# A selective scan in tiles of (state, channel) instead of (channel, state)

## The chip, the cores and the metric

The kernel runs on one core of a Trainium2 chip. The metric is the device time of one execution in microseconds, the median of several runs; for the kernel before it is 7444.82 us over 3 runs (7441.77 to 7446.32). A profiled execution of the same program gives the trace that is read below.

## The reference

Two layers follow each other on an image batch x of shape (4, 128, 128, 128), all in float32. The change lies in the first, a Mamba-like block over the L = 16384 pixels of each image:

```python
h1 = jax.nn.relu(xf @ mlp_w1.T + mlp_b1)
xm = h1 @ mlp_w2.T + mlp_b2
x_in, z = jnp.split(xm @ in_proj_w.T, 2, axis=-1)
u = silu(causal depthwise conv of x_in, 4 taps, + conv_b)      # 256 channels
dt, Bm, Cm = jnp.split(u @ x_proj_w.T, [8, 24], axis=-1)       # 16 states
delta = jax.nn.softplus(dt @ dt_proj_w.T + dt_proj_b)
A = -jnp.exp(A_log)
def step(h, inp):
    d_t, B_t, C_t, u_t = inp
    dA = jnp.exp(d_t[:, :, None] * A)
    h = h * dA + d_t[:, :, None] * B_t[:, None, :] * u_t[:, :, None]
    y = jnp.einsum('bds,bs->bd', h, C_t)
    return (h, y)
y = (ys + u * D) * silu(z)
out = y @ out_proj_w.T          # then group norm over 4 groups, silu, + x
```

So for each of 256 channels d and 16 states s there is a recurrence along the pixels. The second layer (a group norm, a small mixing head, and a filter in the Fourier domain) is not touched.

## The kernel before

`block0` is the first layer, `block1` the second. An image is cut into 32 chunks of T = 512 pixels, so there are 128 chunks for the four images, one after the other. Within a chunk the 256 x 16 = 4096 recurrences are 32 tiles of 128 partitions: a tile holds DG = 32 channels and SQ = 4 states, and partition p is channel p // 4 and state p % 4. Two halves j of 128 channels have four groups of 32 channels each (index m or g) and four groups of four states (index p in the code). A step r of a half takes, for each state group p, the channel group `place(r, p)`, so a step covers all four channel groups, each with another state group.

The recurrence itself is one VectorE instruction per tile along the pixels (L409, a scan of 128x512). It needs two operands:

- da = exp(delta * A), made by ScalarE (L391) from `rdelta`, which holds delta repeated over the four states, with a per-partition scale `amat`.
- b = delta * u * B. For state groups 1 to 3 GpSimd multiplies `rdu` (delta * u repeated over four states) by `rB` (B repeated over 32 channels) into `hb` (L358, `dbu`). For state group 0 it is made on another way: the product du is turned by TensorE so that pixels are on partitions (L288), ScalarE scales it by the four B values of the pixel (L299, `bt_act`, a per-partition scale), which writes the tile `bt`, and TensorE turns a 128-column piece of `bt` back into the PSUM tile b (L378, `dbu_turn`).

The scan result is multiplied by `rC` (C repeated over the channels), on VectorE in place (L411) or on GpSimd (L416), and TensorE sums the four states of each channel with the 0/1 matrix `sel` (L430). ScalarE keeps the last column of each scan for the next chunk (L412, L417).

The repeated tiles come through DRAM. `xd_act` stores B and C as `bc` (L250), `bc_load` reads them back into `rB` and `rC` (L257); `dt_act` stores delta (L272) and `du_pool` stores du (L308) into `dd`, and `rep_load(j)` reads them back into `rdelta` and `rdu` (L315). A load in this kernel fills one group of all 128 partitions, with a source that is repeated: `replicated` repeats each channel's row four times, and `partition_broadcast(DG)` repeats four state rows 32 times. `rB`, `rC`, `rdelta` and `rdu` have two buffers each; `rdelta` and `rdu` are used in turn by the two halves of a chunk.

The order of the work is written out by hand. Time is cut into slots, 16 to a chunk (NP), one for each pair of scans. The list at the end of `pre(k)` and that of `post(k)` give each piece of work of chunk k a slot and a phase, counted from the slot where chunk k - 1 begins its scans; chunk k itself begins at slot 16. In a slot the phases run in the order turn, sums, pe, exps, act, pool, dbu, gate, scans, dve, end. Chunk k's `bc` is stored in slot 4, `rB` and `rC` loaded in slot 5, delta stored in 6, du made and stored in 7, the first half's `rdelta` and `rdu` loaded in 9, and the second half's in 16. `dbu` runs two slots ahead of its scans (the first of a chunk in slot 14), `exps` one slot ahead (15). ScalarE's `bt` work is spread over slots 8 to 14. All these transfers are issued by SP, in that order, from one queue.

For images 0 to 2 the group norm, and after it the mixing head of the second layer (`finish`), run in the chunks of the next image: `norm_load`, `norm_act` and `norm_dve` in 16 of the 32 chunks (L561, L562, L567, L571), `agg_load` and its matmul (L593, L597) in most of the chunks after those.

Of the kernel before, what the change touches and what calls it, by code (L numbers as in the profile page):

```python
# [26 lines left out]
F32 = mybir.dt.float32  # L27
AF = mybir.ActivationFunctionType
# [5 lines left out]
P = 128  # L34
T = 512
DG = 32
SQ = 4
# [8 lines left out]
def kernel(ctx: ExitStack, tc: tile.TileContext, a: dict, out: bass.AP):  # L46
# [91 lines left out]
    stats, outs = {}, {}  # L138
    shared = SimpleNamespace(**{k: v for k, v in locals().items() if k not in ("ctx", "tc")})
    block0(tc, shared)  # L140
    block1(tc, shared)


def block0(tc, s):
    nc, B, NCH, NH, NS, NG, ND, R, NX, KC, HALO, C, L, NF, DI = (
        s.nc, s.B, s.NCH, s.NH, s.NS, s.NG, s.ND, s.R, s.NX, s.KC, s.HALO, s.C, s.L, s.NF, s.DI,
    )
    NT = T // P
    with ExitStack() as ctx:
        def pool(name, bufs, **kw):  # L150
            return ctx.enter_context(tc.tile_pool(name=name, bufs=bufs, **kw))

        p1 = pool("p1", 1)
        p2 = pool("p2", 2)
# [19 lines left out]
        st = {}  # L174
        stats, outs = s.stats, s.outs

        def replicated(ap):

            return ap.rearrange("d (o t) -> d o t", o=1).to_broadcast([DG, SQ, T])

        def pre(k):


# [2 lines left out]
            d = st[k] = {}  # L186
# [65 lines left out]
            def bc_load():  # L252
                for q, tag in enumerate("BC"):
                    t = d[tag] = p2.tile([P, NG - 1 + q, T], F32, tag=f"r{tag}", name=f"r{tag}_{k}")
                    for g in range(1 - q, NG):
                        rows = d["bc"][q, g * SQ : (g + 1) * SQ, :]
                        nc.sync.dma_start(out=t[:, g - 1 + q, :], in_=rows.partition_broadcast(DG))  # L257

            def dt_mm():
                for j in range(NH):  # L260
# [31 lines left out]
            def bt_act(h, n0, n1):  # L292

                if h == n0 == 0:
                    d["bt"] = p2.tile([P, NT, NH * ND, DG, SQ], F32, tag="bt", name=f"bt_{k}")
                for n in range(n0, n1):
                    t, q = divmod(n, SQ)
                    src = ps["dut"][:, 2 * t : 2 * t + 2, :].rearrange("p j (g d) -> p (j g) d", d=DG)
                    nc.scalar.activation(  # L299
                        d["bt"][:, 2 * h + t, :, :, q], src, AF.Copy, scale=d["xdt"][:, 2 * h + t, R + q : R + q + 1]  # L300
                    )

            def du_pool(j):
# [6 lines left out]
            def rep_load(j):  # L310
                for q, tag in enumerate(("delta", "du")):
                    t = d[tag, j] = p2.tile([P, ND, T], F32, tag=f"r{tag}", name=f"r{tag}_{k}_{j}")
                    for g in range(ND):
                        r = j * P + g * DG
                        nc.sync.dma_start(out=t[:, g, :], in_=replicated(d["dd"][q, r : r + DG, :]))  # L315

            return [
                (-9, "pe", load), (-7, "pe", h1_mm), (-6, "act", h1_act), (-5, "pe", xm_mm), (-4, "act", xm_act),
                (-3, "pe", z_mm), (-1, "act", z_act), (0, "pe", partial(cv_mm, 0)), (1, "pe", partial(cv_mm, 1)),
                (2, "act", silu_act), (3, "pe", xd_mm), (4, "act", xd_act), (5, "pe", dt_mm), (5, "pe", xd_turn),  # L320
                (5, "act", bc_load), (6, "act", dt_act), (7, "act", xd_turn_act), (7, "pool", partial(du_pool, 0)),
                (7, "pool", partial(du_pool, 1)), (8, "pe", partial(du_turn, 0)), (9, "act", partial(rep_load, 0)),
                (8, "pool", partial(bt_act, 0, 0, 1)), (9, "act", partial(bt_act, 0, 1, 5)),
                (10, "act", partial(bt_act, 0, 5, 8)), (11, "pe", partial(du_turn, 1)),
                (11, "pool", partial(bt_act, 1, 0, 1)), (12, "act", partial(bt_act, 1, 1, 2)),
                (13, "act", partial(bt_act, 1, 2, 5)), (14, "act", partial(bt_act, 1, 5, 8)),
                (16, "pe", partial(rep_load, 1)),
            ]

# [7 lines left out]
        def place(r, p):  # L337


            return (p - r) % ND  # L340
# [22 lines left out]
        def pair(n):  # L363

            k, r = divmod(n, NP)
            u, p = divmod(r, ND // 2)
            j, r = divmod(u, NG)
            return k, j, r, 2 * p

        def dbu_turn(n):  # L370

            k, j, r, p = pair(n)
            d = st[k]
            if p == 0:
                b = d["b0"] = psd.tile([P, T], F32, tag="b0", name=f"b0_{k}_{j}_{r}")
                for t in range(NT):
                    src = d["bt"][:, t, j * ND + place(r, 0), :, :].rearrange("p d s -> p (d s)")
                    nc.tensor.transpose(b[:, t * P : (t + 1) * P], src, s.ident)  # L378

        def exps(n):  # L380
# [104 lines left out]
        for n in range(n_chunks * NP):  # L485
            todo[n - 1, "exps"].append(partial(exps, n))
            todo[n - 1, "turn"].append(partial(dbu_turn, n))
            todo[n, "scans"].append(partial(scans, n))
            if n % 2 == 0:
                todo[n - 2, "dbu"].append(partial(dbu, n // 2))  # L490
            else:
                todo[n + 2, "sums"].append(partial(sums, n // 2))
# [400 lines left out]
def _layout(inputs):  # L893

    import numpy as np

    v = {k: np.asarray(x) for k, x in inputs.items()}
    p0 = {k[len("L0_conv_"):]: x for k, x in v.items() if k.startswith("L0_conv_")}
    p1 = {k[len("L1_conv_"):]: x for k, x in v.items() if k.startswith("L1_conv_")}
    _, C, H, W = v["x"].shape  # L900
    out = {
        "x": v["x"],
        "mlp_w1T": p0["mlp_w1"].T,
        "mlp_w2T": p0["mlp_w2"].T,
        "in_wT": p0["in_proj_w"].T,
        "conv_wT": p0["conv_w"][:, 0, :].T,

        "alog_q": p0["A_log"].reshape(2, 4, 32, 4, 4).transpose(2, 4, 0, 3, 1).reshape(128, 32),
        "x_wT": p0["x_proj_w"].T,
        "dt_wT": p0["dt_proj_w"].T,  # L910
        "dt_b": p0["dt_proj_b"],
        "out_wT": p0["out_proj_w"].T,
        "agg_wT": p1["agg_w"].T,
        "wg_wT": p1["wg_w"].T,
        "residual_weight": p1["residual_weight"].reshape(1),
    }
    for k in ("mlp_b1", "mlp_b2", "conv_b", "D", "gn_w", "gn_b"):
        out[k] = p0[k]
    for k in ("gn_gamma", "gn_beta", "agg_b", "wg_b", "filt_w"):
        out[k] = p1[k]  # L920

    def groups(n):
        g = np.arange(C) // (C // n)
        return (g[:, None] == g[None, :]) * (n / C)

    def angle(n, rows, cols):
        return 2 * np.pi * ((np.asarray(rows)[:, None] * np.asarray(cols)[None, :]) % n) / n

    h, w, k = np.arange(H), np.arange(W), np.arange(W // 2 + 1)
    ah, aw, ai = angle(H, h, h), angle(W, w, k), angle(W, k, w)  # L930

    half = np.concatenate([h[: H // 2 + 1], H + h[: H // 2 + 1]])
    rows = np.concatenate([h[: H // 2], h[: H // 2 - 1 : -1]])
    out["filt_w"] = out["filt_w"][:, :, rows]
    twice = np.where((k == 0) | (k == W // 2), 1.0, 2.0)[:, None]
    consts = {
        "c_ident": np.eye(C),
        "c_sel": np.repeat(np.eye(32), 4, axis=0),
        "c_g0": groups(4),

        "c_g1": groups(16),
        "c_fh": np.concatenate([np.cos(ah), -np.sin(ah)], 1)[:, half] / np.sqrt(H),
        "c_fwr": np.concatenate([np.cos(aw), -np.sin(aw)], 1) / np.sqrt(W),
        "c_fwi": np.concatenate([np.sin(aw), np.cos(aw)], 1) / np.sqrt(W),
        "c_ihc": np.cos(ah)[rows] / np.sqrt(H),
        "c_ihs": -np.sin(ah)[rows] / np.sqrt(H),
        "c_sign": np.tile(np.repeat([1.0, -1.0], H // 2), (W, 1)),
        "c_iw": np.concatenate([twice * np.cos(ai), -2.0 * np.sin(ai[1:-1])], 0) / np.sqrt(W),
    }
    out |= {k: np.asarray(x, np.float32) for k, x in consts.items()}  # L950
    return {k: np.ascontiguousarray(x) for k, x in out.items()}
# [18 lines left out]
```

## Time and profile before

| | |
|---|---|
| median of 3 runs | 7444.82 us |
| the profiled execution | 7446.74 us |
| its span | 7445.0 us, 90541 instructions |
| DMA packets | 853767, 1242.06 MB |
| VectorE scans (L409), 128x512 | 1268 ns (da from da, st, hb), 1271 ns (h from da, st, b) |
| VectorE product with rC (L411), 128x512 | 674 ns |
| GpSimd product (L358), 128x1536 / 128x1024 / 128x512 | 3447 / 2369 / 1279 ns |
| GpSimd product with rC (L416), 128x1024 | 2367 ns |
| ScalarE exp (L391), 128x512 | 696 ns |
| ScalarE eviction into bt (L299), 128x256 | 708 ns, 2048 of them |
| SP transfers rdelta / rdu / rC / rB | 1024 / 1024 / 512 / 384 of 256 KB |

A busy time counts the instructions of an engine, not its waits; an engine with a high share either sets the pace or stands close to it. A group of instructions shows its number, its total and the mean of one, and then the idle time ahead of them with what ended it. A transfer's time to landing runs from its issue to its completion and holds what was queued ahead of it. The scan stage covers the first 6500 us or so of the span; the second layer's stage is the rest.

### The profile page before, as it was taken

The numbers are of one execution on the slowest core, as the hardware profiler recorded it, in microseconds if no ns is written. First come the engines' busy times: TensorE is split into PE (matmuls) and PEld (weight loads), VectorE is DVE, ScalarE is ACT, GpSimd is POOL, SyncE is SP. The second block draws the span as 40 slices with busy tenths as digits, with TensorE's granted clock in tenths as the row PEclk, the third lists the DMA queues.
The fourth block names the chain that finished last, engine by engine and source line by source line (L and its number), as shares of the span: only waits on it lengthen the run. The fifth ranks groups of instructions, "written<-read, shape, count | busy, mean of one in ns | idle before, by whom it ended". The sixth has DMA issues, their size and how long they took to land.

```text
span 7445.0 us, 90541 instructions
## 1 busy us (share of the span) xinstructions
PE 6005.7 (81%) x25908; PEld 2664.1 (36%) x25908; DVE 7031.4 (94%) x8168; ACT 6328.6 (85%) x13181; POOL 6900.6 (93%) x3188
## 2 busy tenths in 40 slices
PE   7787878877778788887777788877777788867999
PEld 2223223322222233332222223232222233237999
DVE  6999999999999999999999999999999999977787
ACT  6888888888888888888888888888888888866887
POOL 6999999999999999999999999999999999976788
PEclk8888888888888888888888889988888889889999
DMA  4444444444554544544545454445554554547665
GB/s 138 159 154 150 151 156 156 143 161 168 174 188 164 179 165 156 169 166 169 184 168 185 161 171 166 159 165 175 171 188 166 173 169 151 173 149 216 177 185 155
DMA packets 853767, 1242.06 MB, mean 167 GB/s; under 512 B 76680, under 2 KB 308240, under 8 KB 853264
## 3 DMA queue, kind: packets, MB, share of 16 engines
q1 hardware_dynamic: 851152, 1236.11, 50.3%
q8 instruction: 204, 3.34, 0.2%
q14 instruction: 299, 2.45, 0.1%
q10 hardware_dynamic: 2112, 0.16, 0.0%
HBM read 992.71 MB, written 243.27 MB: 166 GB/s over the span
## 4 chain that ended last, share of the span: by engine, by line
ACT 20%; DVE 19%; PE 17%; POOL 9%; issue 8%; DMA 5%; SPq 1%; DVEq 0%; ACTq 0%; POOLq 0%
DVE da L409 8%; ACT da L391 8%; DVE h L409 6%; PE pp_cv L231 5%; ACT bt L299 4%; POOL hb L358 4%; POOL hb L416 4%; DVE hb L411 3%; DMA dd<-delta 2%; PE y L430 2%; PE pa L776 1%; ACT L391 1%; PE px L790 1%; PE px L791 1%; POOL du L307 1%
## 5 line engine op out<-in xcount | busy, mean ns | idle before, releaser
L358 POOL TENSOR_TENSOR hb<-rdu,rB 128x1536 f32<-128x1536 f32 (+2 forms) x1536 | 3607.6, 2365 | 16.2 <-DMA rdu<-dd 16.2
L416 POOL TENSOR_TENSOR hb<-h,rC 128x1024 f32<-128x1024 f32 (+1 forms) x1072 | 2438.7, 2277 | 279.8 <-DVE h L409 263.0
L391 ACT ACTIVATE da<-rdelta,amat 128x512 f32<-128x512 f32 x4096 | 2674.6, 696 | 9.2 <-ACT st L412 0.2
L409 DVE TENSOR_TENSOR_SCAN da<-da,st,hb 128x512 f32<-128x512 f32 x1976 | 2420.3, 1268 | 7.1 <-ACT da L391 7.0
L378 PE MATMUL b<-ident,bt 128*128 128x128 f32 x4096 | 768.9, 311 | 767.9 <-DVE h L409 633.0
L430 PE MATMUL y<-hb,sel 128*32 128x512 f32 x8192 | 1364.0, 743 | 4.8 <-POOL hb L416 2.9
L409 DVE TENSOR_TENSOR_SCAN h<-da,st,b 128x512 f32<-128x512 f32 x992 | 1261.3, 1271 | 111.4 <-POOL hb L358 37.5
L411 DVE TENSOR_TENSOR hb<-da,rC 128x512 f32<-128x512 f32 x2040 | 1296.7, 674 | 3.0
L409 DVE TENSOR_TENSOR_SCAN h<-da,st,hb 128x512 f32<-128x512 f32 x1000 | 1252.7, 1256 | 1.3 <-ACT da L391 1.3
L299 ACT ACTIVATE bt<-pt_dut,xdt 128x256 f32<-128x256 f32 x2048 | 1194.6, 708 | 46.8 <-PE pt_dut L288 46.5
L231 PE MATMUL pp_cv<-xm,wck 128*128 128x512 f32 x2048 | 1111.7, 692 | 9.8 <-ACT zs L225 9.7
L378 PEld LDWEIGHTS b<-ident,bt 128*128 128x128 f32 x4096 | 532.0, 156 | 1341.4 <-DVE h L409 997.1
L412 ACT COPY st<-da 128x1 f32<-128x1 f32 x2040 | 295.8, 173 | 567.9 <-DVE hb L411 562.6
L231 PEld LDWEIGHTS pp_cv<-xm,wck 128*128 128x128 f32 x2048 | 438.4, 226 | 771.1 <-issue 502.8
L755 POOL TENSOR_TENSOR wb<-wb,term 128x1040 f32<-128x1040 f32 x192 | 460.9, 2401 | 157.2 <-ACT term L749 147.2
L288 PE MATMUL pt_dut<-ident,du 128*128 128x128 f32 x1024 | 214.1, 337 | 280.5 <-ACT st L412 271.4
L426 PE MATMUL y<-u,diag 128*128 128x512 f32 x512 | 291.0, 651 | 156.8 <-DVE zs L440 155.6
L307 POOL TENSOR_TENSOR du<-delta,u 128x512 f32<-128x512 f32 x256 | 319.0, 1267 | 37.5 <-ACT delta L270 37.5
L417 ACT COPY st<-h 128x2 f32<-128x2 f32 (+1 forms) x1072 | 214.7, 200 | 162.8 <-DVE h L409 154.6
L288 PEld LDWEIGHTS pt_dut<-ident,du 128*128 128x128 f32 x1024 | 134.1, 164 | 578.6 <-POOL du L307 419.2
L196 PE MATMUL pp_h<-xt,w 128*128 128x512 f32 x512 | 296.6, 707 | 51.7 <-DMA xt<-in_x 46.6
L391 ACT ACT_TABLE_LOAD x261 | 334.9, 1283 | 2.9
(137 smaller groups left out, 8019.0 us busy)
## 6 DMA issues: line engine op xcount, KB each, us to landing
rdelta<-dd SPq DMA_DIRECT2D x1024, 256.0 KB, 3.6
rdu<-dd SPq DMA_DIRECT2D x1024, 256.0 KB, 4.6
rC<-bc SPq DMA_DIRECT2D x512, 256.0 KB, 5.1
rB<-bc SPq DMA_DIRECT2D x384, 256.0 KB, 3.5
dd<-delta SPq DMA_DIRECT2D x256, 256.0 KB, 5.3
dd<-du SPq DMA_DIRECT2D x256, 256.0 KB, 4.5
ft<-in_filt_w SPq DMA_DIRECT2D x96, 520.0 KB, 7.1
xt<-in_x SPq DMA_DIRECT2D x128, 256.0 KB, 5.5
```

Of the source, the lines that this page charges most:

```text
L231: nc.tensor.matmul(ps["cv", j], w, d["xm"][:, t : t + T], start=t == 0, stop=t == KC - 1)
L288: nc.tensor.transpose(ps["dut"][:, 2 * t + j, :], d["du"][:, j, at : at + P], s.ident)
L299: nc.scalar.activation(d["bt"][:, 2 * h + t, :, :, q], src, AF.Copy, scale=d["xdt"][:, 2 * h + t, R + q : R + q + 1])
L307: nc.gpsimd.tensor_tensor(du, d["delta"][:, j, :], d["u"][:, j, :], ALU.mult)
L358: nc.gpsimd.tensor_tensor(hb[:, p : p + n, :], d["du", j][:, m : m + n, :], d["B"][:, p - 1 : p - 1 + n, :], ALU.mult)
L378: nc.tensor.transpose(b[:, t * P : (t + 1) * P], src, s.ident)
L391: nc.scalar.activation(d["da", p][q], d["delta", j][:, m, :], AF.Exp, scale=s.amat[:, c : c + 1])
L409: nc.vector.tensor_tensor_scan(o, das[q], b, init, ALU.mult, ALU.add)
L411: nc.vector.tensor_tensor(hb[:, p + q, :], das[q], d["C"][:, p + q, :], ALU.mult)
L416: nc.gpsimd.tensor_tensor(hb[:, ps, :], h[:, q, :], d["C"][:, ps, :], ALU.mult)
L430: nc.tensor.matmul(y[m * DG : (m + 1) * DG, :], s.sel, d["hb", j, r][:, p, :], start=False, stop=r == NG - 1)
L755: nc.gpsimd.tensor_tensor(wb, wb, u[n].terms[f], ALU.add)
```

## The change

Partition p of a scan tile becomes state p // 32 and channel p % 32: the four states of a group lie in four blocks of 32 partitions. Everything that knows this order follows:

- The loads of `rB`, `rC`, `rdelta` and `rdu` are cut by state, not by group. Each fills the 32 partitions of one state with all groups at once, so that a partition receives four rows of 2 KB (three for `rB`) in place of one. The number of loads of `rdelta`, `rdu` and `rC` stays at four a tile, that of `rB` goes from three to four.
- `bt` has its two innermost dimensions exchanged: `bt_act` writes 32 elements in a row where it wrote elements four apart.
- The turn of `bt` reads the same 128 columns in their new order; the constants `alog_q` (the scale of the exponential) and `c_sel` are laid out for it on the host.

```diff
-        def replicated(ap):
-
-            return ap.rearrange("d (o t) -> d o t", o=1).to_broadcast([DG, SQ, T])
-
@@ bc_load
-                    for g in range(1 - q, NG):
-                        rows = d["bc"][q, g * SQ : (g + 1) * SQ, :]
-                        nc.sync.dma_start(out=t[:, g - 1 + q, :], in_=rows.partition_broadcast(DG))
+                    rows = d["bc"][q, (1 - q) * SQ :, :].rearrange("(g s) t -> s g t", s=SQ)
+                    for m in range(SQ):
+                        nc.sync.dma_start(out=t[m * DG : (m + 1) * DG], in_=rows[m].partition_broadcast(DG))
@@ bt_act
-                    d["bt"] = p2.tile([P, NT, NH * ND, DG, SQ], F32, tag="bt", name=f"bt_{k}")
+                    d["bt"] = p2.tile([P, NT, NH * ND, SQ, DG], F32, tag="bt", name=f"bt_{k}")
...
-                        d["bt"][:, 2 * h + t, :, :, q], src, AF.Copy, scale=d["xdt"][:, 2 * h + t, R + q : R + q + 1]
+                        d["bt"][:, 2 * h + t, :, q, :], src, AF.Copy, scale=d["xdt"][:, 2 * h + t, R + q : R + q + 1]
@@ rep_load
-                    for g in range(ND):
-                        r = j * P + g * DG
-                        nc.sync.dma_start(out=t[:, g, :], in_=replicated(d["dd"][q, r : r + DG, :]))
+                    rows = d["dd"][q, j * P : (j + 1) * P, :].rearrange("(g d) t -> d g t", d=DG)
+                    for m in range(SQ):
+                        nc.sync.dma_start(out=t[m * DG : (m + 1) * DG], in_=rows)
@@ dbu_turn
-                    src = d["bt"][:, t, j * ND + place(r, 0), :, :].rearrange("p d s -> p (d s)")
+                    src = d["bt"][:, t, j * ND + place(r, 0), :, :].rearrange("p s d -> p (s d)")
@@ constants
-        "alog_q": p0["A_log"].reshape(2, 4, 32, 4, 4).transpose(2, 4, 0, 3, 1).reshape(128, 32),
+        "alog_q": p0["A_log"].reshape(2, 4, 32, 4, 4).transpose(4, 2, 0, 3, 1).reshape(128, 32),
...
-        "c_sel": np.repeat(np.eye(32), 4, axis=0),
+        "c_sel": np.tile(np.eye(32), (4, 1)),
```

## The prediction

> **What bounds the kernel now.** First the page's busy times, then the busy time by stretch. The scan stage fills the span up to about 6500 us; its settled part shows (busy us of each engine with its instruction count, granted clock, DMA share, GB/s):
>
> ```profile
> PE 6005.7 (81%) x25908; PEld 2664.1 (36%) x25908; DVE 7031.4 (94%) x8168; ACT 6328.6 (85%) x13181; POOL 6900.6 (93%) x3188
> 100.00:6300.00 6200.00, 4947.85 (x18597) 1828.00 (x18599) 6067.22 (x6376) 5396.32 (x11246) 5944.57 (x2712) 0.86 0.49 166
> ```
>
> There VectorE is busy 6067.22/6200 = 97.9%, GpSimd 95.9%, ScalarE 87.0%. The input transfers of L191 come 121 times, first at 136.1, last at 6283.7 us: 6147.6/120 = 51.2 us a chunk, 3.2 us a slot. So per chunk VectorE idles 133/121 = 1.1 us, GpSimd 255/121 = 2.1, ScalarE 804/121 = 6.6. VectorE bounds; GpSimd is just behind. Next, who makes VectorE wait in that stretch (total us, times, longest):
>
> ```profile
> DVE h L409 <- POOL hb L358: 36.3, 44, 1.2
> DVE h L409 <- POOL du L307: 34.1, 118, 0.6
> DVE h L409 <- POOL hb L416: 30.3, 45, 0.7
> DVE rstd L533 <- ACT rstd L530: 13.0, 6, 2.9
> DVE da L409 <- ACT da L391: 5.9, 8, 1.3
> DVE h L409 <- ACT da L391: 1.3, 3, 0.4
> ```
>
> ScalarE is named for 13.0 + 5.9 + 1.3 = 20.2 us only. Then the groups by shape, for the eviction that changes and for its yardsticks:
>
> ```profile
> L299 ACT ACTIVATE bt<-pt_dut,xdt 128x256 f32<-128x256 f32 x2048 | 1194.6, 708 | 46.8 <-PE pt_dut L288 46.5
> L391 ACT ACTIVATE da<-rdelta,amat 128x512 f32<-128x512 f32 x4096 | 2674.6, 696 | 9.2 <-ACT st L412 0.2 <-DMA rdelta<-dd 0.2
> L749 ACT ACTIVATE term<-ft,wts 128x1040 f32<-128x1040 f32 x192 | 221.2, 1152 | 1.7 <-DMA ft<-in_filt_w 1.7
> ```
>
> Half the elements of L391 take as long. Last, SP's queue in one plain chunk, then GpSimd's first use of the du that it loads:
>
> ```profile
> 684.39 1.81 SPq L257 DMA_DIRECT2D rB<-bc  x3
> 686.32 2.47 SPq L257 DMA_DIRECT2D rC<-bc  x4
> ...
> 693.53 2.46 SPq L315 DMA_DIRECT2D rdelta<-dd  x4
> 696.10 2.48 SPq L315 DMA_DIRECT2D rdu<-dd  x4
> ...
> 710.23 3.44 POOL L358 TENSOR_TENSOR hb<-rdu,rB 128x1536 f32<-128x1536 f32 x1
> ```
>
> The fourth rdu is issued near 697.9 and takes 4.9 us to land: 702.8, 7.4 us before 710.23. In a chunk of the normalizing pass the same reading gives 2544.2 against 2551.57 (7.4), in one that also reloads x1 3052.4 against 3058.47 (6.1). This slack is what the change can use up. The transfer rates, in stretches of one kind (length, two columns to skip, DMA share, GB/s):
>
> ```profile
> 2522.20:2522.30 0.10, 1.00 1.10 246
> 2533.00:2536.00 3.00, 0.50 1.04 400
> 713.00:719.90 6.90, 0.54 0.88 298
> 685.60:691.30 5.70, 1.00 0.92 280
> ```
>
> In order: the bc store out of 32 partitions; plain 128-partition transfers; replicated rdelta and rdu; rB and rC.
>
> [...]
>
> **The change part by part.**
>
> *bt, removed stride.* Between L391 and L749 an element costs (1152 - 696)/(1040 - 512) = 0.864 ns, so 256 in a row cost 696 - 256 x 0.864 = 475 ns.[...] I take 480; the ends are 400 and 708 (no gain). 2048 x 228 ns = 467 us off ScalarE, 16 x 0.228 = 3.6 us a chunk. It is mostly worth nothing, since ScalarE already waits for VectorE at L412 and L417. It can return at most the 20.2 us; the 13.0 belong to a chain of small steps, so I take 5 us gained, from 0 to 20.
>
> *Loads by state, moved.* Before, each load covers 128 partitions with one 2 KB row; now 32 partitions with four rows (three for rB). Bytes are the same. rdelta, rdu and rC keep four transfers of 0.262 MB; rB goes from three of 0.262 to four of 0.197, so SP issues one more a chunk, 0.6 us on a queue that is mostly waiting. The list of the built program shows no other added or moved instruction. Each transfer waits for the one eight places ahead of it, as before.
>
> Rate: the 32-partition store moves 246/400 = 0.615 of the plain rate; scaled for busy shares, (246/1.10)/(400/1.04) = 0.58. 0.58 x 298 = 173 GB/s if the two limits multiply; 246/1.10 = 224[...] I take 205, from 172 to 224.[...]
>
> On the path to rdu are 7 x 0.262 = 1.835 MB of rB and rC and 8 x 0.262 = 2.097 MB of rdelta and rdu. Before: 1.835/0.280 + 2.097/0.298 = 6.6 + 7.0 = 13.6 us. After: 3.932/0.205 = 19.2, that is 5.6 us later (4.0 at 224, 9.3 at 172). The slack is 6.1 to 7.4, so hidden at 205. Past it GpSimd can lose another 2.1 us a chunk, its idle time, and VectorE scans hb only at 717.10, 3.4 us after the product ends at 713.67.
>
> *What is queued behind.* The delta and du stores and xt follow rC: about 1.835/0.205 - 6.6 = 2.4 us later. xt feeds L196, which PE meets before the next transpose of b: in the chunk near 3044 that transpose ends at 3047.85 and VectorE wants b at 3052.36, 4.5 us spare, so hidden. Without cover, PE's delay would reach VectorE one for one. The second set of rdelta and rdu needs 2.097/0.205 - 7.0 = 3.2 us more and is used over 10 us after it lands: hidden. rB and rC are double-buffered by chunk and used 17 us after rC lands: hidden.
>
> *Waits.* A reader of one group now waits for all four loads. The first product with rC in a chunk (L411) waits for four transfers at once where two products waited for one each. GpSimd's first product already carries four or five such waits with no idle time beside the start-up 16.2 us, so I price this at 0; if each new multiple wait cost 0.28 us, the size of VectorE's stop beside du (34.1/118), it would be 128 x 0.28 = 36 us.
>
> *Transposes, sel and amat* only change their order of rows: 0, same shapes.
>
> *Start.* Nothing covers the first loads: GpSimd waits for rdu until 56.58, its product takes 3.4, and VectorE's second scan starts at 62.10, 2.1 us after that. 5.6 us later leaves +4 us, from 0 to 9.
>
> Sum: profiled execution 7446.74 (span 7445.0), -5 + 4 = 7445.7. It lies 1.9 above the median of 7444.82, so the forecast is 7444.
>
> **The rivals.**
>
> *A: loads hidden*, as above, 7444.
>
> *B: late loads, slower.* [...]rdu misses GpSimd's slot, and GpSimd, with 2.1 us to spare, drags VectorE. It starts to cost where the lateness passes 6.1 + 2.1 us in the 42 chunks that reload x1 (rate under 3.932/21.8 = 180), and 7.4 + 2.1 in the other 86 (under 170). At 172 the first lose 9.3 - 8.2 = 1.1 us: 46 us, 7490. At 160 the delay is 11.0: 86 x 1.5 + 42 x 2.8 = 247 us, about 7690. For it: the ratio 0.58. Against: DMA share 0.49, the gap after 702.
>
> *C: the wait of several transfers, or xt, stops VectorE.* 36 us: 7480. For it: VectorE has no slack. Against: no idle time at GpSimd's like waits.
>
> *D: faster.* ScalarE holds 20% of the chain that ended last, L299 4%. If its relief also ended half of the 100.7 us for which VectorE is shown waiting on GpSimd: 7444 - 15 - 50 = about 7380; with the 20.2 alone, 7429. Against: these waits name GpSimd.
>
> *That the change doesn't do what it says:* bt stays near 708 ns. Then 7449, still A.
>
> **How the numbers follow.** 0.2%, about 15 us, is what a measurement of this kernel can tell from no change. A 0.42, within 0.2%; B 0.28 and C 0.14, slower; D 0.16, faster. A's own range is 7430 to 7458. The range over all starts at 7428, leaving out the better half of D (0.07), and ends at 7600, where B's rate would be about 164 GB/s; beyond lies 0.12.
>
> **What would show it.** Right: L299 at 450 to 500 ns; ScalarE idle 3 us more a chunk; rdu landing later by 4 to 7 us, GpSimd's L358 without waits for it; DMA share of the scan stage up from 0.49 to about 0.6; VectorE still near 98%. Wrong: L358 waiting on rdu in every chunk, VectorE's L409 on L358 (B); idle time ahead of L411 or L409 with transfers or PE named (C); VectorE's waits on GpSimd gone (D).

## The result and the profile after

The changed kernel takes 7413.87 us, the median of 8 runs (7407.25 to 7423.48), against 7439.61 (8 runs, 7435.95 to 7446.32) of the kernel before: a ratio of 0.9965, with an interval of 0.9957 to 0.9974. It is faster by 0.35%. The forecast was 7444 with a range from 7428, so the time lies 14 us below the range, between the two prices given for rival D. The profiled execution took 7411.48 us with a span of 7409.7, against 7446.74 and 7445.0: 35.3 us less.

The page of the kernel after: the busy times, the DMA queue that moves the data, three groups by shape and an issue (KB each, median us from issue to landing). L405, L295 and L192 are L409, L299 and L196 of before.

```profile
PE 5982.2 (81%) x25908; PEld 2690.3 (36%) x25908; DVE 7033.2 (95%) x8168; ACT 6082.8 (82%) x13181; POOL 6896.5 (93%) x3188
...
q1 hardware_dynamic: 853200, 1236.11, 68.1%
...
L405 DVE TENSOR_TENSOR_SCAN h<-da,st,b 128x512 f32<-128x512 f32 x992 | 1262.2, 1272 | 73.8 <-POOL du L303 33.6 <-POOL hb L412 22.5 <-ACT da L387 5.0
...
L295 ACT ACTIVATE bt<-pt_dut,xdt 128x256 f32<-128x256 f32 x2048 | 834.5, 469 | 146.2 <-PE pt_dut L284 146.2
...
L192 PE MATMUL pp_h<-xt,w 128*128 128x512 f32 x512 | 398.0, 922 | 285.3 <-DMA xt<-in_x 259.5 <-ACT st L408 21.0 <-ACT da L387 4.8
...
rdu<-dd SPq DMA_DIRECT2D x1024, 256.0 KB, 7.8
```

The lines of before for the b scan, the matmuls on xt and the load of rdu, which were not shown with the prediction:

```profile
L409 DVE TENSOR_TENSOR_SCAN h<-da,st,b 128x512 f32<-128x512 f32 x992 | 1261.3, 1271 | 111.4 <-POOL hb L358 37.5 <-POOL du L307 34.1 <-POOL hb L416 30.3
...
L196 PE MATMUL pp_h<-xt,w 128*128 128x512 f32 x512 | 296.6, 707 | 51.7 <-DMA xt<-in_x 46.6 <-ACT da L391 4.8
...
rdu<-dd SPq DMA_DIRECT2D x1024, 256.0 KB, 4.6
```

And the settled stretch after, in the form of the prediction's second line:

```profile
100.00:6300.00 6200.00, 4954.33 (x18683) 1866.30 (x18682) 6097.29 (x6406) 5185.46 (x11295) 5967.88 (x2725) 0.85 0.69 166
```

Both halves of the change are there. The eviction into bt fell from 708 to 469 ns. The same 1236 MB now keep the 16 DMA engines busy for 68.1% of the span and not 50.3%; a load of rdu lands 7.8 us after its issue and not 4.6, and one of xt after 7.5 and not 5.5. VectorE's busy time is unchanged (7031.4 and 7033.2). What is gone is idle time ahead of one form, the scan whose b comes through TensorE: 111.4 us before, 73.8 after. That is 37.6 us, and the span became 35.3 shorter. In the stretch VectorE idles for 6200 - 6097.29 = 102.7 us, where it was 132.8.

Who VectorE waits for in the settled stretch from 100 to 6300 us, after (total us, times, longest):

```profile
DVE h L405 <- POOL du L303: 33.7, 117, 0.5
DVE h L405 <- POOL hb L412: 22.5, 35, 1.5
DVE rstd L529 <- ACT rstd L526: 12.0, 6, 3.1
DVE h L405 <- ACT da L387: 10.1, 16, 1.9
DVE h L405 <- POOL hb L354: 6.7, 9, 1.4
```

The row that stood first before, the wait for GpSimd's product hb of L358 (36.3 us in 44 stops), is down to 6.7 us in 9 stops (a new row of that name, ahead of the da scan, holds 5.0 us in 6). The waits that name ScalarE did not shrink: those for da rose from 7.2 us (5.9 and 1.3) to 12.1 (10.1 and a smaller row of 2.0). A cheaper ScalarE instruction took away stops that the profile puts down to GpSimd, although GpSimd's work was not changed.

### The profile page after: what moved, and what is told of

It reads as the page before. It is cut to its first block, busy times and chain, and to the rows that moved or that the text cites. A ratio compares the mean times of both kernels' runs of the same rounds, so it can differ in the third digit from the quotient of the medians.

```text
span 7409.7 us, 90629 instructions
## 1 busy us (share of the span) xinstructions
PE 5982.2 (81%) x25908; PEld 2690.3 (36%) x25908; DVE 7033.2 (95%) x8168; ACT 6082.8 (82%) x13181; POOL 6896.5 (93%) x3188
## 3 DMA queue, kind: packets, MB, share of 16 engines
q1 hardware_dynamic: 853200, 1236.11, 68.1%
## 5 line engine op out<-in xcount | busy, mean ns | idle before, releaser
L354 POOL TENSOR_TENSOR hb<-rdu,rB 128x1536 f32<-128x1536 f32 (+2 forms) x1536 | 3604.4, 2363 | 32.9 <-DMA rdu<-dd 28.9
L412 POOL TENSOR_TENSOR hb<-h,rC 128x1024 f32<-128x1024 f32 (+1 forms) x1072 | 2436.1, 2275 | 235.3 <-DVE h L405 217.4
L405 DVE TENSOR_TENSOR_SCAN da<-da,st,hb 128x512 f32<-128x512 f32 x1976 | 2421.6, 1269 | 7.3 <-POOL hb L354 5.3
L426 PE MATMUL y<-hb,sel 128*32 128x512 f32 x8192 | 1332.5, 726 | 2.9 <-POOL hb L412 2.7
L405 DVE TENSOR_TENSOR_SCAN h<-da,st,b 128x512 f32<-128x512 f32 x992 | 1262.2, 1272 | 73.8 <-POOL du L303 33.6
L407 DVE TENSOR_TENSOR hb<-da,rC 128x512 f32<-128x512 f32 x2040 | 1298.0, 676 | 3.0
L405 DVE TENSOR_TENSOR_SCAN h<-da,st,hb 128x512 f32<-128x512 f32 x1000 | 1254.6, 1258 | 5.7 <-ACT da L387 5.7
L227 PE MATMUL pp_cv<-xm,wck 128*128 128x512 f32 x2048 | 1051.1, 660 | 35.6 <-ACT zs L221 34.7
L374 PEld LDWEIGHTS b<-ident,bt 128*128 128x128 f32 x4096 | 563.4, 160 | 1147.7 <-DVE h L405 746.5
L295 ACT ACTIVATE bt<-pt_dut,xdt 128x256 f32<-128x256 f32 x2048 | 834.5, 469 | 146.2 <-PE pt_dut L284 146.2
L408 ACT COPY st<-da 128x1 f32<-128x1 f32 x2040 | 280.5, 161 | 644.6 <-DVE hb L407 638.7
L227 PEld LDWEIGHTS pp_cv<-xm,wck 128*128 128x128 f32 x2048 | 412.9, 213 | 739.0 <-issue 464.1
L192 PE MATMUL pp_h<-xt,w 128*128 128x512 f32 x512 | 398.0, 922 | 285.3 <-DMA xt<-in_x 259.5
L387 ACT ACT_TABLE_LOAD x261 | 334.9, 1283 | 2.9
```

The costliest lines, as they stand in the source:

```text
L192: nc.tensor.matmul(ps["h", j], s.w1[:, j * P : (j + 1) * P], d["xt"], start=True, stop=True)
L227: nc.tensor.matmul(ps["cv", j], w, d["xm"][:, t : t + T], start=t == 0, stop=t == KC - 1)
L295: nc.scalar.activation(d["bt"][:, 2 * h + t, :, q, :], src, AF.Copy, scale=d["xdt"][:, 2 * h + t, R + q : R + q + 1])
L354: nc.gpsimd.tensor_tensor(hb[:, p : p + n, :], d["du", j][:, m : m + n, :], d["B"][:, p - 1 : p - 1 + n, :], ALU.mult)
L387: nc.scalar.activation(d["da", p][q], d["delta", j][:, m, :], AF.Exp, scale=s.amat[:, c : c + 1])
L405: nc.vector.tensor_tensor_scan(o, das[q], b, init, ALU.mult, ALU.add)
```

## Why the stops named after GpSimd are ScalarE's

One of these stops, in the timeline of the kernel before (start, length, engine, instruction, idle time with its releaser), with what leads to it in the same chunk:

```profile
308.61 1.66 ACT L299 ACTIVATE bt<-pt_dut,xdt 128x256 f32<-128x256 f32 x3
...
310.33 0.47 PE L378 MATMUL b<-ident,bt 128*128 128x128 f32 x1 [1.25 <-ACT st L417]
...
312.60 5.64 PE L231 MATMUL pp_cv<-xm,wck 128*128 128x512 f32 x8
...
320.49 1.28 ACT L236 ACT_TABLE_LOAD   x1
323.34 0.69 ACT L236 ACTIVATE u<-pp_cv,conv_b 128x512 f32<-128x512 f32 x1 [0.86 <-PE pp_cv L231]
...
325.06 1.28 ACT L391 ACT_TABLE_LOAD   x1
326.35 1.30 ACT L391 ACTIVATE da<-rdelta,amat 128x512 f32<-128x512 f32 x2
327.16 1.28 DVE L409 TENSOR_TENSOR_SCAN h<-da,st,b 128x512 f32<-128x512 f32 x1 [1.00 <-POOL hb L358]
```

VectorE stops for 1.00 us before the scan at 327.16, and the last releaser named is GpSimd's L358. But the scan begins 0.81 us after ScalarE began its two exponentials at 326.35: the first of them (0.72 us in the record of the trace) and 0.09 more. In 43 of the 44 stops that name L358 in the settled stretch the distance is 0.81 us, while the product of L358 that is named ended between 0.05 and 1.01 us before the scan. (In the 44th, at 4264.65, the turn of b ended last.) Of the 118 stops that name GpSimd's L307, 117 have the same 0.81 us (the exponentials start at 3605.81, the scan at 3606.62). In these the du product ended some 0.15 us before the scan too, nearly as steadily, so that only experiment 7 tells the two apart. The stops that name L416 are another matter: there a scan at 1977.82 starts 0.04 us after a product of L416 ends at 1977.78, and so in all 45, so these are GpSimd's.

ScalarE is late here because the silu waited 0.86 us for the convolution (323.34), and with table loads of 1.28 us on both sides (at 320.49 and 325.06) it holds back the exponentials. The convolution is late because of what stands ahead of it in TensorE's order of work (its 6252 groups of matmuls follow each other in one and the same order in this trace and in that of the changed kernel): the last of the four pieces of the first turn of b in this chunk needs the last three bt evictions, which end at 310.27, and it starts at 310.33 (the profile names another releaser there too). Behind it stand the y sums (1.94 us from 310.73) and the convolution, whose second half starts at 319.60.

So this became the **queue theory**: late bt, then the first turn of b, the y sums and the convolution, the silu between two table loads, the exponentials, VectorE. Its rivals: a **work theory** (ScalarE is late from the amount of its work, so that any relief counts, wherever it falls) and a **GpSimd theory** (the names are right, and GpSimd gains from the loads or from something else in the change). The same places of a chunk after the change, to be counted from 3047.05, where VectorE's b scan three steps earlier starts (307.20 in the chunk above):

```profile
3049.81 0.33 PE L374 MATMUL b<-ident,bt 128*128 128x128 f32 x1 [0.89 <-ACT bt L295]
...
3051.65 4.76 PE L227 MATMUL pp_cv<-xm,wck 128*128 128x512 f32 x8
...
3061.64 1.27 ACT L232 ACTIVATE u<-pp_cv,conv_b 128x512 f32<-128x512 f32 x2
...
3065.23 1.30 ACT L387 ACTIVATE da<-rdelta,amat 128x512 f32<-128x512 f32 x2
3066.04 1.28 DVE L405 TENSOR_TENSOR_SCAN h<-da,st,b 128x512 f32<-128x512 f32 x1
```

The first convolution starts 4.60 us after the mark and not 5.40. Its eight matmuls take 4.76 us and not 5.64. The second starts 10.73 us after the mark and not 12.40. The silu runs without a break, and the scan follows its exponential by the same 0.81 us, now with no stop ahead of it. (That very chunk in the kernel before, marked at 3058.26, has 5.58, 5.59 and 12.53 us, and VectorE stops for 1.13 us at 3078.35.)

Why the same eight matmuls take 5.64, 4.76 or 3.70 us can be read from the granted clock, which the profile gives as a share of TensorE's full clock. The two convolutions of the chunk above in the kernel before, then the first of the chunk after the change (length, busy us of PE, PEld, DVE, ACT and POOL, granted clock, DMA share, GB/s):

```profile
312.60:318.24 5.64, 5.64 (x14) 2.54 (x11) 5.64 (x6) 2.92 (x7) 5.64 (x3) 0.65 0.74 237
319.60:323.30 3.70, 3.70 (x14) 1.73 (x11) 3.70 (x5) 2.84 (x4) 3.70 (x3) 1.00 0.00 0
...
3051.65:3056.41 4.76, 4.76 (x14) 2.23 (x11) 4.76 (x6) 2.89 (x8) 4.76 (x3) 0.77 1.06 217
```

In the kernel before the clock is 0.50 from 309.70 to 316.53, and from 306.20 to 309.70 TensorE had worked for only 0.55 us (at 308.53). So of the 1.80 us that the second convolution of the same chunk gains (12.53 to 10.73), about 0.98 is the queue moving up and 0.83 the first convolution at a higher clock. The matmuls are no other: 3.70/0.65 = 5.7 and 3.70/0.77 = 4.8 us.

## Experiments

All times stand beside the kernel before, measured on the same chip with each group of runs (medians from 7440.7 to 7444.03 us); a ratio has its 95% interval.

**1. The eviction alone.** The kernel before with bt in rows; loads and constants stay.

```diff
-                    d["bt"] = p2.tile([P, NT, NH * ND, DG, SQ], F32, tag="bt", name=f"bt_{k}")
+                    d["bt"] = p2.tile([P, NT, NH * ND, SQ, DG], F32, tag="bt", name=f"bt_{k}")
...
-                        d["bt"][:, 2 * h + t, :, :, q], src, AF.Copy, scale=d["xdt"][:, 2 * h + t, R + q : R + q + 1]
+                        d["bt"][:, 2 * h + t, :, q, :], src, AF.Copy, scale=d["xdt"][:, 2 * h + t, R + q : R + q + 1]
...
-                    src = d["bt"][:, t, j * ND + place(r, 0), :, :].rearrange("p d s -> p (d s)")
+                    src = d["bt"][:, t, j * ND + place(r, 0), :, :].rearrange("p s d -> p (s d)")
```

> The kernel before with bt alone changed: ScalarE writes 32 elements in a row and the turn reads the same 128 columns; loads and constants stay, so that the first state group's products are paired with the wrong channels and states. Queue theory (a late bt holds TensorE's turn of b, the convolution behind it, silu, and then the exponentials that VectorE waits for): 7400 to 7412 us, ratio 0.9945 to 0.9965; L299 near 470 ns; VectorE's stops that the trace puts to L358, 37.5 us before, under 10. Work theory (ScalarE's saved time counts in proportion to its share): the same ratio. GpSimd theory (those stops are GpSimd's, and the new shape of the loads ended them): 1.000, stops stay near 37.

Measured: 7402.51 us, 0.9949 [0.9936, 0.9961], with the eviction at 467 ns. VectorE's waits in the settled stretch:

```profile
DVE h L409 <- POOL du L307: 34.1, 118, 0.7
...
DVE h L409 <- POOL hb L358: 6.4, 11, 1.1
```

The eviction alone gives the whole gain, and 11 us more than the change has (the two intervals overlap a little). With that the view falls that these stops wait for GpSimd: no instruction of GpSimd and no load changed.

**2. The loads alone.** The changed kernel's loads and constants, bt strided as before (the three lines above left out).

> The changed kernel with bt written and read four apart as before, so only the loads, sel and amat are new; the first state group's products are paired wrongly. Queue and work theory: nothing gained and the start later by 4 to 6 us: 7443 to 7455, ratio 1.0005 to 1.002, and 708 ns for the eviction into bt. GpSimd theory: the gain of the change, ratio near 0.9965.

Measured: 7484.79 us, 1.0058 [1.0045, 1.0071]. That is 44 us slower, and all three expectations missed it. GpSimd's wait for rdu is small there too (8.5 us in 9 stops). VectorE's and TensorE's waits in the settled stretch and TensorE's group that needs xt:

```profile
DVE h L405 <- POOL hb L354: 33.9, 34, 1.2
...
DVE h L405 <- ACT da L387: 18.5, 23, 1.3
...
L192 PE MATMUL pp_h<-xt,w 128*128 128x512 f32 x512 | 379.7, 883 | 278.9 <-DMA xt<-in_x 278.9
```

VectorE's waits for ScalarE's da went from 7.2 to 26.9 us (18.5, and 8.4 ahead of the other scan), while those named L354 hardly moved, and TensorE stands 278.9 us ahead of the matmuls on xt, where it stood 51.7. Another 7.7 us in 14 stops name the turn of b itself. This pointed at xt, which is queued behind rB and rC (experiments 9 to 12).

**3 and 4. Half of the evictions.** bt in rows for the second half of a chunk only (evictions of slots 11 to 14), and for the first half only (slots 8 to 10). Both halves shorten the same number of evictions on ScalarE.

```diff
+                    o = rows[:, 2 * h + t, :, q, :] if h == 1 else step[:, 2 * h + t, :, :, q]
...
-                        d["bt"][:, 2 * h + t, :, :, q], src, AF.Copy, scale=d["xdt"][:, 2 * h + t, R + q : R + q + 1]
+                        o, src, AF.Copy, scale=d["xdt"][:, 2 * h + t, R + q : R + q + 1]
```

(`rows` and `step` are two views of the same tile; experiment 4 has `h == 0`.)

> The kernel before with only the second half of the evictions into bt (slots 11 to 14) written in a row; that half's products are paired wrongly. Queue theory: all of the gain, 0.9945 to 0.9965, since only these stand ahead of the turn of b. Work theory: half of it, near 0.998. GpSimd theory: 1.000.

> The kernel before with only the first half of the evictions into bt (slots 8 to 10) written in a row; that half's products are paired wrongly. Queue theory: nothing, 0.9993 to 1.0005, because ScalarE waits for VectorE between the halves. Work theory: near 0.998. GpSimd theory: 1.000.

Measured: second half 7402.42 us, 0.9949 [0.9937, 0.9962]; first half 7438.49 us, 0.9998 [0.999, 1.0006]. The mean eviction is 587 and 590 ns. In the second kernel VectorE's first wait is what it was (its lines are shifted by 4):

```profile
DVE h L413 <- POOL hb L362: 35.4, 43, 1.4
```

ScalarE's busy time falls by 138 us in experiment 3 and by 104 in 4. A like relief of ScalarE gives all of the gain in one place and none in the other. It is not ScalarE's amount of work that counts, but when the last evictions end.

**5. The same slow eviction, a slot earlier.** The kernel before, bt strided; only the slots of the second half's evictions change.

```diff
-                (11, "pool", partial(bt_act, 1, 0, 1)), (12, "act", partial(bt_act, 1, 1, 2)),
-                (13, "act", partial(bt_act, 1, 2, 5)), (14, "act", partial(bt_act, 1, 5, 8)),
+                (11, "pool", partial(bt_act, 1, 0, 1)), (12, "act", partial(bt_act, 1, 1, 5)),
+                (13, "act", partial(bt_act, 1, 5, 8)),
```

> The kernel before with the evictions into bt as slow as they were (708 ns), but the second half's last six put one slot earlier (four evictions in slot 12, three in 13, none in 14). Queue theory: the turn of b and the convolution come earlier, the stops put to L358 fall from 37.5 us to under 10, ratio 0.9945 to 0.997. Work theory: same work, 1.000. GpSimd theory: 1.000.

Measured: 7409.05 us, 0.9953 [0.994, 0.9965], with the eviction at 712 ns. So a kernel that saves nothing on ScalarE gains what the change gains. VectorE's wait on L358, and the convolution's matmuls:

```profile
DVE h L409 <- POOL hb L358: 2.7, 6, 0.7
...
L231 PE MATMUL pp_cv<-xm,wck 128*128 128x512 f32 x2048 | 965.1, 614 | 184.7 <-ACT zs L225 184.6
```

A matmul takes 614 ns here, 692 before and 660 after. TensorE even stands longer just ahead of the convolution (184.7 us in all, 9.8 before), but the mean granted clock of the settled stretch is 0.91 and not 0.86. So part of this gain too is clock. The longer stand just ahead went with a higher clock here; which stands lower it was not isolated.

**6 and 7. The far end of the chain.** One activation function replaced by Relu, which takes table loads with it; the values change. First silu, then softplus (L270). ScalarE has 159 and 255 instructions fewer than the 13181 before; its table loads of 1283 ns at L391 fall from 261 to 182 and to 134.

```diff
-                    nc.scalar.activation(u[:, j, :], ps["cv", j], AF.Silu, bias=s.cb[:, j : j + 1])
-                nc.scalar.activation(d["zs"], d["zs"], AF.Silu)
+                    nc.scalar.activation(u[:, j, :], ps["cv", j], AF.Relu, bias=s.cb[:, j : j + 1])
+                nc.scalar.activation(d["zs"], d["zs"], AF.Relu)
```

> The kernel before with Relu in place of Silu for u and zs (L236, L237), which leaves out the function that needs another table and with it the table loads of that slot; the values are other ones. If the stops put to L358 are ScalarE's: they go, ratio 0.994 to 0.996. If they are GpSimd's: 37 us of them stay, 0.999 to 1.000.

> The kernel before with Relu in place of Softplus for delta (L270), which leaves out those table loads; the values are other ones. If the stops put to GpSimd's du (L307, 34.1 us, about 0.29 each) are ScalarE's: they go, ratio 0.9945 to 0.996. If they are GpSimd's: they stay, 0.999 to 1.000.

Measured: without silu 7410.71 us, 0.9956 [0.9942, 0.9969]; without softplus 7389.81 us, 0.9927 [0.9914, 0.9939]. VectorE's first waits, without silu and then without softplus:

```profile
DVE h L409 <- POOL du L307: 34.1, 118, 0.6
...
DVE h L409 <- POOL hb L358: 2.2, 6, 0.7
```

```profile
DVE h L409 <- POOL hb L416: 48.5, 46, 1.6
...
DVE h L409 <- POOL hb L358: 13.8, 26, 1.2
```

Without silu the L358 stops go and those of L307 stay whole. Without softplus the L307 stops go, those of L358 become fewer (13.8 us in 26), and those of L416, which are GpSimd's, grow from 30.3 to 48.5 us. The removal also settles the one case that the distances left open. Without softplus each of the 118 scans that stopped for L307 starts before its du product ends, by 0.19 to 0.39 us, and none of them stops. One of them, where the first of the two products ends near 2196.96:

```profile
2195.69 2.49 POOL L307 TENSOR_TENSOR du<-delta,u 128x512 f32<-128x512 f32 x2
...
2196.76 1.27 DVE L409 TENSOR_TENSOR_SCAN h<-da,st,b 128x512 f32<-128x512 f32 x1
```

So these scans do not need du at all. Both names are GpSimd's and both causes ScalarE's: the exponentials stand behind the silu in one place and behind the softplus in the other. Without softplus the kernel gains 54 us where the expectation had at most 41. VectorE idles 38.4 us less in the settled stretch and its busy time is 12.0 us lower (7031.4 to 7019.4); why the latter was not traced.

**8. Both cures of the eviction.** The changed kernel with the second half's evictions a slot earlier, as in 5.

> The changed kernel with the second half's evictions into bt put one slot earlier as well. Queue theory: TensorE's last wait for bt (0.9 us in a chunk) goes too, the stops that are left (6.7 us put to L354) shrink: ratio 0.995 to 0.9965 against the kernel before, at best 8 us under the changed kernel. Work theory: as the changed kernel, 0.9965.

Measured: 7406.71 us, 0.9953 [0.9941, 0.9966]. The intervals of this, of experiment 5 and of the change overlap, and the work theory's 0.9965 lies inside this one, so the run does not tell the theories apart. It only fits the view that two cures of one wait hardly add up.

**9. xt earlier, in the changed kernel.** Its load leaves slot 7 for slot 4, ahead of rB and rC on SP's queue.

```diff
-                (-9, "pe", load), (-7, "pe", h1_mm), (-6, "act", h1_act), (-5, "pe", xm_mm), (-4, "act", xm_act),
+                (-12, "pe", load), (-7, "pe", h1_mm), (-6, "act", h1_act), (-5, "pe", xm_mm), (-4, "act", xm_act),
```

> The changed kernel with the input tile xt loaded in slot 4 of its chunk, ahead of bc, rB and rC in SP's queue, in place of slot 7 behind them. If the slower loads cost what they cost because xt comes late and TensorE stands before L192 (259.5 us in all): that wait falls under 60 us and the time to that of bt alone plus the later start: 7402 to 7410, ratio 0.995 to 0.996. If they cost it through rdu: 7412 to 7416, no change.

Measured: 7397.8 us, 0.9939 [0.9926, 0.9951], faster than either expectation. TensorE's wait goes and the pace of those matmuls returns:

```profile
L192 PE MATMUL pp_h<-xt,w 128*128 128x512 f32 x512 | 302.0, 718 | 6.8 <-DMA xt<-in_x 6.8
```

16 us come back over the change (7413.87 to 7397.8), and the intervals are apart. So VectorE does pay for where xt stands, although no row of its waits names it. Not all of the 16 us need be the lateness that the loads brought: the eviction alone, with the loads of before and xt in slot 7, takes 7402.51, which is 5 us more (those two intervals overlap). The eviction alone with an early xt was not run.

**10 and 11. xt earlier with the slow eviction.** In experiment 2, and in the kernel before.

> The kernel with only the loads new (bt as slow as before, first state group paired wrongly), and xt loaded in slot 4. If xt is the loads' cost: most of the 0.58% comes back, 7443 to 7455, ratio 1.000 to 1.002. If rdu or the waits of several transfers are it: 7475 to 7490, ratio 1.0045 to 1.007.

> The kernel before with xt loaded in slot 4 and nothing else. In the kernel with only the loads new, xt early gave back 13 of 44 us; no wait for a transfer is left there, and new stops stand in the chunks that reload x1, where TensorE idles after an early L192 and then runs slowly. If that idling is the rest of the loss: 7455 to 7475, ratio 1.001 to 1.004, with new stops in the same chunks (2600 to 3250 us). If the rest is the loads': 7436 to 7446, ratio 0.999 to 1.0005.

Measured: the loads alone with xt early 7471.95 us, 1.0041 [1.0028, 1.0054], between the two expected ranges; the kernel before with xt early 7467.97, 1.0033 [1.002, 1.0045], as expected if TensorE's idling costs. Only 13 of the 44 us came back, and the second run shows why: with the slow eviction an early xt costs 24 us by itself, with the loads of before. From 2600 to 3250 us VectorE has 19 stops that name L358 where it had 7. Compared at the same place of xt, the loads cost 4.0 us, which the overlapping intervals do not tell from nothing. In the first of the two, one of its new stops in a chunk that reloads x1:

```profile
2645.83 1.94 PE L426 MATMUL y<-hb,sel 128*32 128x512 f32 x8
...
2648.85 0.73 ACT L295 ACTIVATE bt<-pt_dut,xdt 128x256 f32<-128x256 f32 x1 [1.45 <-PE pt_dut L284]
2649.63 1.30 ACT L387 ACTIVATE da<-rdelta,amat 128x512 f32<-128x512 f32 x2
...
2650.41 1.29 DVE L405 TENSOR_TENSOR_SCAN da<-da,st,hb 128x512 f32<-128x512 f32 x1 [0.73 <-POOL hb L354]
```

Again the name is GpSimd's, and the scan follows ScalarE's exponential by 0.78 us. ScalarE stood 1.45 us waiting for TensorE, whose y sums took 1.94 us; in the chunk of before eight of them take 1.94 at a granted clock of 0.50 (at 310.73) and 1.06 at 1.00 (at 324.53). The slow eviction (0.73 us at 2648.85) then stands ahead of the exponential. Why an early xt makes these places worse while the eviction is slow was not isolated.

**12. Both cures together.** The changed kernel with xt early (9) and the evictions early (5).

> The changed kernel with xt loaded in slot 4 and the second half's evictions into bt one slot earlier. If both causes are right: 7395 to 7405, ratio 0.994 to 0.9955, under both kernels. If either is wrong: as the changed kernel with bt early, 0.9953, or above.

Measured: 7393.93 us, 0.9933 [0.9919, 0.9947], a little below the expected range. It beats both kernels: 49 us below the kernel before, 20 below the change. Its interval overlaps that of experiment 9, so what the early evictions add to an early xt is not shown.

## Why the prediction was wrong

- **bt.** Predicted 480 ns between 400 and 708; 469. Right. The step from there to "467 us off ScalarE" was too large: evictions in a row overlap. Three took 1.66 us before (at 308.61), where three times the mean of 708 ns are 2.12, and 1.18 after (at 3048.57), 0.16 us less each, the group's busy time fell by 360 us (1194.6 to 834.5) and ScalarE's by 246; in the settled stretch it idles 1.7 us more a chunk, where 3 was named as a sign. For the end it did not matter.
- **"It can return at most the 20.2 us ... so I take 5 us gained".** This step failed. It read "who makes VectorE wait" by the names in the trace, and took the 36.3 us of L358 and the 34.1 of L307 as GpSimd's. They were ScalarE's, as the fixed 0.81 us and experiments 1, 6 and 7 show. By these rows ScalarE could return 20.2 + 36.3 + 34.1 = about 91 us and not 20.2, and the last evictions held most of the 36.3 of L358. The eviction measured by itself returned 38 us (experiment 1), where 5 was taken.
- **The place of bt.** The prediction spread its 3.6 us a chunk over ScalarE as if all 16 evictions counted alike. Experiments 3 and 4 put the whole worth into those of the second half, through TensorE's order of work and the clock that it was granted. The trace of before held this: the last piece of the first turn of b started 0.06 us after the last eviction.
- **Loads by state.** The rate was well taken: rdelta and rdu move at 220 and 209 GB/s in two stretches after the change (699 to 706 us, 712.5 to 720.5), where 205 was taken, from 172 to 224. The ends lie where the rates of before put them (0.58 x 298 = 173, 246/1.10 = 224); 205 between them was the author's estimate. rdu landed 3.2 us later by its own median time to landing (4.6 to 7.8), on top of which come the loads ahead of it; the predicted 5.6 us later is the sum over both. It was hidden, as predicted: GpSimd's L354 waited for rdu 7.2 us in 11 stops of the whole stretch. DMA share of the stretch was predicted at about 0.6 and is 0.69.
- **"xt ... so hidden".** Wrong: in the changed kernel up to 16 us hang on it (experiment 9). The lateness was well sized (2.4 us predicted; time to landing 5.5 to 7.5). The step compared it with the spare 4.5 us of one transpose in one chunk. It missed that the matmuls on xt then ran at 922 and not 707 ns, and that everything in TensorE's order moves with them. The clock again: of those that ran at one granted clock throughout, 273 of 416 ran at a granted clock of 0.50 after the change, and 42 of 414 before (settled stretch).
- **Start.** Predicted +4 us. GpSimd's first L358 comes at 61.16 and not 56.58, 4.6 us later, against 5.6 worked out. VectorE's busy time in the first 100 us is 37.55 us, 37.78 before and 42.13 with the eviction alone: the loads took back there the 4.4 us that the eviction gave. These terms do not simply add: with the loads alone it is no lower than before (38.46). At an early xt the loads take 3.8 us there (42.16 to 38.40), which is about all that they cost in those two runs (4.0).
- **Waits of several transfers, transposes, sel, amat, SP's extra issue.** No new idle time ahead of L407 or L412, and none ahead of L354 that names several transfers; 0, as taken.

By terms: eviction -38, loads about +11 beside it (7402.5 to 7413.9), of which some 5 at the start and the rest, as far as experiment 9 shows, with xt. The sum of the two predicted terms, -5 and +4, was off mostly in the first. The rival that came true is D, with 0.16: "if its relief also ended half of the 100.7 us". What ended is about a third: the row of L358 fell by 30 us. D was set low because "these waits name GpSimd", and this is the sentence that the runs overturned. A was right that rdu is hidden and wrong in its total; B went, as no rdu was late enough; of C no wait of several transfers showed, but xt did cost.

## What to carry to other kernels

When an instruction waits for several engines, test the releaser the profile names: list its stops and look for the event that stands at the same distance before each start. A varying distance clears the engine named. A constant one makes a suspect only, since everything that follows from one cause keeps step: here ScalarE's first exponential, but in one family of stops also GpSimd's product and in the other a matmul of TensorE (L242, begun 0.75 us ahead in 43 of the 44 stops) that these scans do not read. Take the producer of an operand, and then move it alone and see whether the stop moves. Price a faster instruction by its last use in the order of work of the engine that needs it rather than by its share of work: here half of the evictions held all of the gain, and moving them by one slot was worth about as much as making them faster. Compare the granted clock in the same places before and after: here it made up nearly half of what the convolution gained. When a load is slowed, follow what is queued behind it on the same queue to the engine that meets it first, and ask whether that engine will idle there (here TensorE: 46.6 us ahead of the matmuls on xt before, 259.5 after).

## What the hardware showed beyond the expectation

- TensorE's matmuls of one shape had different paces with the granted clock. Eight convolution matmuls took 5.64 us at 0.65 and 3.70 at 1.00 later in the same chunk; the mean was 692 ns before, 660 after and 614 with the evictions early; the xt matmuls took 922 ns with 259.5 us of waiting for the load ahead of them (after) and 718 with 6.8 (experiment 9). Of those after the change that ran at one clock throughout (settled stretch), the median is 1061 ns at 0.50 and 592 at 1.00. The clock fell to 0.50 at 309.70 within a stand of 1.25 us (ahead of 310.33), with one of 2.33 just before and 0.55 us of work between; what stand is enough was not isolated.
- Loads that fill 32 partitions with four rows each kept the DMA engines busy 1.35 times as long for the same bytes (68.1% against 50.3% of nearly equal spans), and yet they cost only 4.0 us, within the noise, when xt was not queued behind them (experiments 10 and 11, with the slow eviction).
- A scan that waits only for the first of two exponentials started 0.81 us after that pair began, in 160 of the 162 stops of the settled stretch that name L358 or L307: 0.72 us for the exponential and 0.09 from its end to the scan.
